# A two-layer attention kernel: the second scores of a layer-0 row placed behind the attention product of the row before

## The chip, the cores and the metric

The kernel runs on one core of one Trainium2 chip. Its engines are named as the profile names them: PE (TensorE, the matrix engine) with PEld (its weight loads), DVE (VectorE), ACT (ScalarE), POOL (GpSimd) and SP (SyncE, which issues most DMAs). The metric is the device time of one execution in microseconds (us). Beside plain timed runs there is one profiled execution, in which every instruction has a start and an end; its "span" is the time from the first to the last instruction.

## What is computed

The input x has 128 rows of 256 tokens with 256 channels, all float32. Two attention layers follow each other, each on a group-normalised copy of its input and with a residual. Layer 0, the one that is changed here, has 8 heads of 32 channels:

```python
bias = jnp.einsum('nijz,zh->nhij', pair_repr, bias_proj)[:, None]
gate = jax.nn.sigmoid(msa_repr @ gate_proj).reshape(bs, s, r, head, c)
q, k, v = jnp.split(msa_repr @ qkv_proj, 3, axis=-1)
...
sim = jnp.einsum('nsqhc,nskhc->nshqk', q, k) * scale
sim = jax.nn.softmax(sim, axis=-1)
sim = sim + bias
attend = jnp.einsum('nshqk,nskhc->nsqhc', sim, v) * gate
out = attend.reshape(bs, s, r, cm) @ out_proj
```

The bias is added after the softmax. So the attention output of a row is the sum of two products with v: the softmax weights with v, and the bias with v. Layer 1 has 4 heads of 64 channels and looks only at keys within 16 tokens of the query; the change doesn't touch it.

## The kernel before

The kernel has three stages: an early one (statistics of x, the bias table, weights turned into place), layer 0, and layer 1. Layer 0 goes row by row, `s` from 0 to 128 (lines 823 to 850), as a software pipeline: in step `s` the scores of row `s` are made, the attention of row `s - 1` is finished, and the projections of a later pair of rows are made.

Inside `tc.manual_schedule` (line 814) the order in which the source issues instructions is the order on PE, ACT and DVE; POOL and SP are not in its list. In a step PE gets, in order:

- `scores(s, 0)`: the scores of heads 0 to 3. Each product has 32 channels to sum over and 128 keys by 256 queries to write, a tile of 32x128 of PE's array ("32\*128" in the profile), and four heads stand side by side. Eight products, 16 matmul instructions (a float32 product is two passes), written `sim`, line 702. ACT then takes four exponentials (`ex`, line 713), each 128x512.
- `sum_heads(s - 1)`: the softmax sums of the row before (`zs`, line 743, 8 products) and the product of the bias with v (`bv`, line 729, 16 products). These sum over 128 keys and write 32 channels: tiles of 128x32 ("128\*32").
- `scores(s, 1)`: heads 4 to 7, as the first.
- `attend(s - 1)`: the product of the exponentials with v (`av`, line 729 too, 16 products), 128x32 tiles again. DVE then forms `at` (lines 774 to 777) from `bv`, `av`, the sums `z` and the reciprocal `d` that `divide` prepared.
- `stretch(...)`: the projections of a pair of rows with whole-array products ("128\*128"): q and k in even steps, v and the gate in odd ones. Each of the two (`f` and `g` in `sevens`, line 595) is made by seven products of half matrices instead of eight, accumulated in its own PSUM bank and copied out by ACT in between: product 1 and 5 and a copy "15" (line 580), product 2 of both into a shared bank (`twos`), then products 3, 6, 7, 4 with further copies. Product 3 accumulates onto what copy "15" has to have read. Between the last of these the output projection of row `s - 1` (`po`, line 634) is interleaved; it needs `at`.

PSUM has eight banks. Three are for `z`, `bv` and `av`; the other five are one ring (line 329, `psum(banks0, "0", 5, 0)`), from which the score tiles `sim`, the banks of the stretch and `po` are taken in turn: four sims, four sims, f's bank, g's bank, the shared bank, po. So each takes over the bank that was handed out five places earlier: f's bank was that of the last sim of `scores(s, 0)`, g's bank and the shared bank were those of the first and second sim of `scores(s, 1)`, and the first sim of `scores(s, 1)` takes that of the `po` of the step before, which DVE's sum into `o` (line 788) has to have read.

ACT's order in a step is: four exponentials of `scores(s, 0)`, the copy of `zs` into `z` (line 756), in even steps the exponential of the gate (line 831), four exponentials of `scores(s, 1)`, then the copies of the stretch. DVE's order is: one join of exponentials (line 719), `d` and its reciprocal (lines 758 and 759), the three operations of `at`, the other three joins, the minimum of z, the normalisation of a later row, and the output sum `o` with its statistics.

Of the kernel before, what the change touches and what calls it, by code (L numbers as in the profile page):

```python
# [39 lines left out]
def conv_preact_kernel(  # L40
# [608 lines left out]
    with ExitStack() as both:  # L649
# [6 lines left out]
        def load1(g):  # L656
            if g * XG < S and g not in ygs:
                yg = big1.tile([P, XG, 2, R], F32, tag="yg", name=f"yg{g}", bufs=5)
                nc.sync.dma_start(out=yg, in_=rows(x1, g * XG, XG))
                ygs[g] = yg  # L660

        with ExitStack() as lay0:
            row = lay0.enter_context(tc.tile_pool(name="row0", bufs=2))
            att = lay0.enter_context(tc.tile_pool(name="att0", bufs=2))
            st, hd, outs = {}, {}, {}
# [5 lines left out]
            def normal(s):  # L671
                if s >= S:
                    return
                g, k = ROWS[s]
                if k == 0:
                    load(g + 1)
                xt = row.tile([P, 2, R], F32, tag="xt", name=f"xt{s}", bufs=6)
                turned(xt, xgs[g], k)
                st[s] = {"xt": xt}
                i, r = divmod(s, 2)  # L680
                if r == 0:
                    xns[i] = row.tile([P, 4, R], F32, tag="xn", name=f"xn{i}")
                for half in range(2):
                    nc.vector.tensor_scalar(  # L684
                        xns[i][:, 2 * r + half, :], xt[:, half, :],
                        mean0[:, half : half + 1], rstd0[:, half : half + 1],
                        op0=ALU.subtract, op1=ALU.mult,
                    )

            def sum_rows(i):  # L690
                if 2 * i < S:
                    tss[i] = row.tile([P, 4, R], F32, tag="ts", name=f"ts{i}", bufs=1)
                    row_sums(tss[i], xns[i])

            def scores(s, half):
                i, r = divmod(s, 2)
                q, k = res["q", i], res["k", i]
                sims = [sim_bank(f"sim{s}_{half}_{j}") for j in range(4)]
                for kt in range(2):
                    for j in range(4):  # L700
                        p0 = D0 * j
                        nc.tensor.matmul(  # L702
                            sims[j][:, kt, :],
                            lhsT=k[p0 : p0 + D0, 2 * r + half, kt * P : (kt + 1) * P],
                            rhs=q[p0 : p0 + D0, 2 * r + half, :],
                            start=True, stop=True,
                        )
                ex = att.tile([P, 4, 2, R], F32, tag="ex", name=f"ex{s}_{half}", bufs=4)
                both = att.tile([P, 4, R], F32, tag="both", name=f"both{s}_{half}")
                hd[s, half] = (ex, both)  # L710

                for j in range(4):
                    nc.scalar.activation(ex[:, j], sims[j], AF.Exp, scale=1.0 / math.sqrt(D0))  # L713

            def join_tiles(s, half, j):

                if s < S:
                    ex, both = hd[s, half]
                    nc.vector.tensor_tensor(both[:, j : j + 2], ex[:, j : j + 2, 0, :], ex[:, j : j + 2, 1, :], ALU.add)  # L719

            def products(to, s, weights):

                i, r = divmod(s, 2)
                v = res["v", i]
                for half in range(2):
                    for kt in range(2):
                        for j in range(4):
                            c0 = kt * P + j * D0
                            nc.tensor.matmul(  # L729
                                to[D0 * j : D0 * (j + 1), half, :],  # L730
                                lhsT=v[:, 2 * r + half, c0 : c0 + D0], rhs=weights(4 * half + j, kt),
                                start=(kt == 0), stop=(kt == 1),
                            )

            def sum_heads(s):
                if s < 0:
                    return
                zs = ps_av.tile([P, 2, R], F32, tag="z", name=f"zs{s}")
                bv0 = ps_av.tile([P, 2, R], F32, tag="bv", name=f"bv{s}")
                for half in range(2):  # L740
                    both = hd[s, half][1]
                    for j in range(4):
                        nc.tensor.matmul(  # L743
                            zs[D0 * j : D0 * (j + 1), half, :], lhsT=ones[:, 0:D0], rhs=both[:, j, :],
                            start=True, stop=True,
                        )
                products(bv0, s, lambda h, kt: bias_sb[:, kt, h, :])
                hd[s] = bv0
                return zs
# [12 lines left out]
            def least(s, z):  # L762
                if s >= 0:
                    nc.vector.tensor_reduce(zmin[:, s : s + 1], z, axis=AX.XY, op=ALU.min)

            def attend(s):
                if s < 0:
                    return
                (ex0, _), (ex1, _), bv0 = hd.pop((s, 0)), hd.pop((s, 1)), hd.pop(s)
                av = ps_av.tile([P, 2, R], F32, tag="av", name=f"av{s}")  # L770
                products(av, s, lambda h, kt: (ex0, ex1)[h // 4][:, h % 4, kt, :])
                z, d = hd.pop((s, "z"))
                t = att.tile([P, 2, R], F32, tag="t", name=f"t{s}", bufs=1)
                nc.vector.tensor_tensor(t, bv0, z, ALU.mult)
                nc.vector.tensor_tensor(t, av, t, ALU.add)
                at = row.tile([P, 2, R], F32, tag="at", name=f"at{s}", bufs=1)
                nc.vector.tensor_tensor(at, t, d, ALU.mult)  # L777
                st[s]["at"] = at
# [18 lines left out]
            def stretch(names, i, s):  # L797

                po = iter(())
                if s >= 0:  # L800
                    po = one_by_one(out_sb, st[s]["at"], f"po{s}", lambda ps: st[s].update(po=ps))
                if 2 * i >= S:
                    for _ in po:
                        pass
                    return
                f, g = (
                    Seven(row, quarters[w], xns[i], tss[i], f"{w}{i}", w, by_token=(w == "v")) for w in names
                )
                for w, p in zip(names, (f, g)):
                    res[w, i] = p.to  # L810
                sevens(row, f, g, f"{names}{i}", po)


            with tc.manual_schedule(engines={mybir.EngineType.PE, mybir.EngineType.Activation, mybir.EngineType.DVE}):
                for s in range(2):
                    normal(s)
                sum_rows(0)
                stretch("qk", 0, -1)
                for s in range(2, 4):
                    normal(s)  # L820
                stretch("vg", 0, -1)
                sum_rows(1)
                for s in range(S + 1):
                    if s < S:
                        scores(s, 0)
                    zs = sum_heads(s - 1)
                    join_tiles(s, 0, 0)
                    divide(s - 1, zs)
                    if s % 2 == 0 and s < S:
                        e = res["g", s // 2]  # L830
                        nc.scalar.activation(e, e, AF.Exp, scale=-1.0)
                    if s < S:
                        scores(s, 1)
                    z = hd[s - 1, "z"][0] if s > 0 else None
                    attend(s - 1)
                    for half, j in ((0, 2), (1, 0), (1, 2)):
                        join_tiles(s, half, j)
                    least(s - 1, z)
                    if s == 4:
                        for weights in quarters1.values():  # L840
                            weights.sum()
                    if s == S - 1:
                        most1 = join_most(st1, stats1, 1)
                        load1(0)
                        load1(1)
                    stretch(("qk", "vg")[s % 2], s // 2 + 1, s - 1)
                    normal(s + 4)
                    if s % 2 == 1:
                        sum_rows((s + 3) // 2)
                    finish(s - 1)  # L850
# [6 lines left out]
        with ExitStack() as lay:  # L857
# [3 lines left out]
            st, hd, outs = {s: {} for s in range(S)}, {}, {}  # L861
# [403 lines left out]
```

## Time and profile before

| | us |
|---|---|
| median of 3 runs | 3258.2 |
| lowest and highest | 3253.23 and 3259.37 |
| profiled execution | 3257.72 |
| its span | 3256.0 |

The groups of the profile that belong to the lines concerned (the columns after the name: shapes, count, then busy us and mean ns of one instruction, then idle time of the engine before it and what ended it):

```profile
L713 ACT ACTIVATE ex<-sim 128x512 f32<-128x512 f32 x1024 | 527.4, 601 | 249.8 <-PE sim L702 249.8
...
L702 PE MATMUL sim<-q,k 32*128 32x256 f32 x4096 | 295.7, 401 | 1.1 <-ACT ex L713 1.1
...
L729 PE MATMUL av<-ex,v 128*32 128x256 f32 x4096 | 247.5, 382 | 0.0
...
L729 PE MATMUL bv<-bias_sb,v 128*32 128x256 f32 x4096 | 244.5, 379 | 0.0
```

A timeline of the profile merges like instructions that follow each other: its columns are the start, the time from the first start to the last end, the engine, the line, the operation, the tiles written and read, the form, the number of instructions, and in brackets the idle time before it and what ended that.

### The profile page before, as it was taken

Reading aid. Unit: us, or ns where it says so; the run is one execution under the profiler, and the core shown is the slowest. Engines: PE = TensorE matmul, PEld = TensorE weight load, DVE = VectorE, ACT = ScalarE, POOL = GpSimd, SP = SyncE. Lnnn points to the kernel's source line nnn. Section 1 sums busy time; section 2 is a strip of 40 time slices with the busy share of each in tenths; the row PEclk is TensorE's granted clock in tenths of the full one; section 3 lists DMA queues with packets and bytes.
Section 4 is the critical chain, followed back from the end, with each engine's and each line's share of the span. In section 5 each row is a group of like instructions: output and inputs, shape, how many; then the busy total and the mean of one; then the engine's idle time right before and its main releaser. Section 6 shows DMA issues by size and latency. Waiting matters only on the chain.

```text
span 3256.0 us, 86773 instructions
## 1 busy us (share of the span) xinstructions
PE 3151.5 (97%) x36937; PEld 2442.3 (75%) x36937; DVE 2678.8 (82%) x3547; ACT 2041.1 (63%) x4306; POOL 1683.4 (52%) x1657
## 2 busy tenths in 40 slices
PE   6799999999999999999999999799999999999997
PEld 4567777777777777777777777588888888888886
DVE  4759999999999999999999999857777777776667
ACT  4566666666666666666666666466666666665663
POOL 3034444444444444444444444287777777776774
PEclk9999999999999999999999999899999999999999
DMA  9931111111111111111111110012222222222221
GB/s 386 414 89 53 53 34 41 35 39 34 40 37 37 34 40 37 37 34 40 40 34 37 37 40 27 21 28 63 57 67 67 67 55 65 67 67 53 61 59 48
DMA packets 346330, 209.36 MB, mean 64 GB/s; under 512 B 273608, under 2 KB 339152, under 8 KB 339664
## 3 DMA queue, kind: packets, MB, share of 16 engines
q1 hardware_dynamic: 345040, 201.37, 21.2%
q8 instruction: 292, 4.78, 0.6%
q0 software_dynamic: 752, 2.36, 0.2%
q14 instruction: 102, 0.84, 0.1%
q10 hardware_dynamic: 144, 0.00, 0.0%
HBM read 136.59 MB, written 67.11 MB: 63 GB/s over the span
## 4 chain that ended last, share of the span: by engine, by line
PE 92%; DMA 3%; DVE 3%; issue 1%; ACT 0%; POOL 0%; SPq 0%; DVEq 0%; ACTq 0%
PE sim L702 8%; PE p1v L917 7%; PE av L729 7%; PE 1po L634 7%; PE po L634 7%; PE bv L729 7%; PE pv L569 6%; PE pq L565 6%; PE p1q L565 5%; PE pk L565 5%; PE p1k L565 5%; PE pg L565 5%; PE zs L743 4%; DMA xs<-in_x_dram 3%; PE 1sim L938 3%; PE 1avz L970 2%
## 5 line engine op out<-in xcount | busy, mean ns | idle before, releaser
L998 DVE RECIPROCAL 1rz<-1z 128x512 f32<-128x512 f32 x128 | 427.8, 3342 | 319.5 <-ACT 1z L992 319.5
L713 ACT ACTIVATE ex<-sim 128x512 f32<-128x512 f32 x1024 | 527.4, 601 | 249.8 <-PE sim L702 249.8
L719 DVE TENSOR_TENSOR both<-ex 128x512 f32<-128x512 f32 x512 | 484.1, 984 | 77.9 <-ACT ex L713 77.9
L759 DVE RECIPROCAL d<-d 128x512 f32<-128x512 f32 x128 | 429.2, 3353 | 4.4
L592 POOL TENSOR_TENSOR v<-v,twovg 128x256 f32<-128x256 f32 x64 | 72.8, 1137 | 551.3 <-ACT twovg L608 551.3
L634 PE MATMUL po<-at,out_sb 128*128 128x256 f32 x1024 | 288.3, 385 | 12.1 <-DVE at L777 12.1
L702 PE MATMUL sim<-q,k 32*128 32x256 f32 x4096 | 295.7, 401 | 1.1 <-ACT ex L713 1.1
L634 PE MATMUL 1po<-1at,w_out_t 128*128 128x256 f32 x1024 | 271.5, 389 | 5.0 <-DVE 1at L1004 3.1
L702 PEld LDWEIGHTS sim<-q,k 32*128 32x128 f32 x4096 | 186.6, 184 | 102.4 <-issue 69.4
L729 PE MATMUL av<-ex,v 128*32 128x256 f32 x4096 | 247.5, 382 | 0.0
L948 POOL TENSOR_TENSOR 1p<-1ex,seen 128x768 f32<-128x768 f32 x128 | 232.7, 1818 | 23.3 <-ACT 1ex L946 23.3
L729 PE MATMUL bv<-bias_sb,v 128*32 128x256 f32 x4096 | 244.5, 379 | 0.0
L917 PEld LDWEIGHTS p1v<-w_in_t,1xn 128*64 128x64 f32 x4096 | 223.6, 137 | 22.0 <-issue 22.0
L917 PE MATMUL p1v<-w_in_t,1xn 128*64 128x128 f32 x4096 | 239.1, 275 | 1.1 <-DVE 1xn L883 1.1
L634 PEld LDWEIGHTS 1po<-1at,w_out_t 128*128 128x128 f32 x1024 | 191.1, 192 | 54.6 <-ACT 1z L992 20.4
L634 PEld LDWEIGHTS po<-at,out_sb 128*128 128x128 f32 x1024 | 187.9, 194 | 34.4 <-issue 7.7
L592 POOL TENSOR_TENSOR q<-q,twoqk 128x256 f32<-128x256 f32 x64 | 47.2, 737 | 298.5 <-ACT twoqk L608 298.5
L729 PEld LDWEIGHTS av<-ex,v 128*32 128x32 f32 x4096 | 120.1, 109 | 108.2 <-issue 42.1
L729 PEld LDWEIGHTS bv<-bias_sb,v 128*32 128x32 f32 x4096 | 133.1, 110 | 87.9
L684 DVE TENSOR_SCALAR xn<-xt,mean,rstd 128x256 f32<-128x256 f32 x256 | 196.8, 808 | 0.0
L593 POOL TENSOR_TENSOR 1q<-1q,mid1q 128x512 f32<-128x512 f32 x64 | 81.6, 1274 | 191.2 <-ACT 1q L589 191.2
L955 POOL TENSOR_TENSOR 1zp<-1p 128x512 f32<-128x512 f32 x128 | 162.6, 1270 | 10.0
(259 smaller groups left out, 7638.3 us busy)
## 6 DMA issues: line engine op xcount, KB each, us to landing
pr<-in_L_conv_pair_repr_dram SPq DMA_DIRECT2D x32, 1024.0 KB, 22.9
x<-o SPq DMA_DIRECT2D x64, 512.0 KB, 2.8
yg<-x SPq DMA_DIRECT2D x64, 512.0 KB, 4.3
out_dram<-1o SPq DMA_DIRECT2D x256, 128.0 KB, 4.3
xg<-in_x_dram SPq DMA_DIRECT2D x252, 128.0 KB, 3.1
xs<-in_x_dram SPq DMA_DIRECT2D x15, 2048.0 KB, 21.8
xs<-in_x_dram SPq DMA_DIRECT2D x2, 1024.0 KB, 17.5
qkv_sb<-in_L_conv_qkv_proj_dram POOLq DMA_DIRECT2D x4, 192.0 KB, 12.2
```

The lines of the kernel that those rows point to most:

```text
L565: nc.tensor.matmul(out, lhsT=weights, rhs=moving, start=first, **flags)
L569: nc.tensor.matmul(out[:, cols], lhsT=moving[:, cols], rhs=weights, start=first and t2 == 0, **flags)
L634: nc.tensor.matmul(ps[:, m, :], lhsT=w[:, kt, m * P : (m + 1) * P], rhs=at[:, kt, :], start=(kt == 0), stop=(kt == 1),)
L684: nc.vector.tensor_scalar(xns[i][:, 2 * r + half, :], xt[:, half, :], mean0[:, half : half + 1], rstd0[:, half : half + 1], op0=ALU.subtra ...
L702: nc.tensor.matmul(sims[j][:, kt, :], lhsT=k[p0 : p0 + D0, 2 * r + half, kt * P : (kt + 1) * P], rhs=q[p0 : p0 + D0, 2 * r + half, :], sta ...
L713: nc.scalar.activation(ex[:, j], sims[j], AF.Exp, scale=1.0 / math.sqrt(D0))
L719: nc.vector.tensor_tensor(both[:, j : j + 2], ex[:, j : j + 2, 0, :], ex[:, j : j + 2, 1, :], ALU.add)
L729: nc.tensor.matmul(to[D0 * j : D0 * (j + 1), half, :], lhsT=v[:, 2 * r + half, c0 : c0 + D0], rhs=weights(4 * half + j, kt), start=(kt == ...
L759: nc.vector.reciprocal(d, d)
L917: nc.tensor.matmul(ps[KB * half : KB * (half + 1), b, :], lhsT=xns[i][:, 2 * r + kt, KB * b : KB * (b + 1)], rhs=w_in_t[:, kt, 2 * C + P * ...
L948: nc.gpsimd.tensor_tensor(p.rearrange("p j (r c) -> p (j r) c", c=WROW)[:, :, 0 : 2 * WSTEP] .rearrange("p r (t c) -> p r t c", c=WSTEP)[: ...
L998: nc.vector.reciprocal(st[s]["rz"], st[s]["z"])
```

## The change

Two calls in the step of layer 0 change places: `attend(s - 1)` is called ahead of `scores(s, 1)`. The line that looks up `z` moves along, since `attend` takes the entry out of its table. Nothing else is changed.

```diff
                     if s % 2 == 0 and s < S:
                         e = res["g", s // 2]
                         nc.scalar.activation(e, e, AF.Exp, scale=-1.0)
+                    z = hd[s - 1, "z"][0] if s > 0 else None
+                    attend(s - 1)
                     if s < S:
                         scores(s, 1)
-                    z = hd[s - 1, "z"][0] if s > 0 else None
-                    attend(s - 1)
                     for half, j in ((0, 2), (1, 0), (1, 2)):
                         join_tiles(s, half, j)
                     least(s - 1, z)
```

## The prediction

> **What bounds the kernel now.** First the page: the span, the engines, and the chain of work that ended last.
>
> ```profile
> span 3256.0 us, 86773 instructions
> PE 3151.5 (97%) x36937; PEld 2442.3 (75%) x36937; DVE 2678.8 (82%) x3547; ACT 2041.1 (63%) x4306; POOL 1683.4 (52%) x1657
> ...
> PE 92%; DMA 3%; DVE 3%; issue 1%; ACT 0%; POOL 0%; SPq 0%; DVEq 0%; ACTq 0%
> ```
>
> TensorE is the chain for 92% of the span. Two views then narrow it to the stage that is changed, layer 0 from its second row on (221 to 2080 us): the busy time of that stretch, and PE's waits in it.
>
> ```profile
> 221.00:2080.00 1859.00, 1855.62 (x19504) 1359.22 (x19503) 1732.01 (x2001) 1206.00 (x2451) 808.70 (x750) 1.00 0.14 37
> ```
>
> ```profile
> PE po L634 <- DVE at L777: 3.4, 1, 3.4
> ```
>
> The columns are PE, PEld (weight loads), DVE, ACT, POOL. PE is without a matmul for 3.4 us in 1859, and that is one wait at the stage's end. So time can come only from inside what counts as PE busy. The timeline of PE over one even row shows where (start, length, then the group; each 128x256 product is two passes):
>
> ```profile
> 1004.41 1.15 PE L702 MATMUL sim<-q,k 32*128 32x256 f32 x16
> 1005.48 1.07 PE L743 MATMUL zs<-both,ones 128*32 128x256 f32 x16
> 1006.37 1.91 PE L729 MATMUL bv<-bias_sb,v 128*32 128x256 f32 x32
> 1008.21 1.15 PE L702 MATMUL sim<-q,k 32*128 32x256 f32 x16
> 1009.28 1.93 PE L729 MATMUL av<-ex,v 128*32 128x256 f32 x32
> 1011.15 0.70 PE L565 MATMUL pq<-xn,qkv_sb 128*128 128x256 f32 x2
> 1011.68 0.59 PE L565 MATMUL pq<-ts,sums_q 128*128 128x256 f32 x2
> 1012.12 0.59 PE L565 MATMUL pk<-xn,qkv_sb 128*128 128x256 f32 x2
> ...
> 1013.84 0.59 PE L565 MATMUL pq<-xn,sums_q 128*128 128x256 f32 x2
> ```
>
> Read starts, not lengths, since lengths overlap. Undisturbed, two passes take 0.432 (1011.68 to 1012.12), so one takes 0.216, and four small tiles side by side take the time of one. That gives an ideal for each group, from its start to the next start. zs: 4 passes, 0.86, took 0.89. bv: 8 passes, 1.73, took 1.84. Each sim: 0.86, took 1.07 and 1.07. av: 1.73, took 1.87. The first pq: 0.43, took 0.53. The excess stands only where the tile form changes: about 0.11 on leaving a form, and on entering one 0.02 (128x32) or 0.10 (32x128 and 128x128). There are five changes in a row of 14.71 us (1004.41 to the next row's start at 1019.12).
>
> **What the Trainium skill says.** "TensorEngine Tiling (Array Packing)", section "Tiling Modes", says that a change of tiling mode, not of tile alone, drains TensorE. The trace agrees and gives the price: bv follows zs in the same mode without excess, every change costs about 0.13 to 0.21. "TensorE: Matmul & The Clock Gate", Part 2, says that a next weight load is pulled ahead of running matmuls; here the timeline of weight loads agrees inside a mode (pk's at 1011.90, its matmul at 1012.12), and at a change shows the loader idle 0.33 to 0.41 before it and the load uncovered. "Perfetto Trace Analysis", on the tensor engine's instructions, says that PE's end times are modelled; hence starts.
>
> **The change part by part.** The built programs show PE's order alone altered: sim(0), zs, bv, av, sim(1), stretch. DVE, ACT, POOL and SP issue the same instructions in the same order, so no instruction or DMA is added or passed over on any of them. It acts in rows 1 to 127 (row 0 has no av, row 128 no scores).
>
> 1. One mode change goes. Before, bv, sim(1), av take 1.84 + 1.07 + 1.87 = 4.78. After: bv 1.73, since av follows in its mode; av 1.73 + 0.11 for leaving to sim = 1.84; sim(1) 1.07, if leaving to the 128x128 products costs what leaving to av did; together 4.64. pq's own 0.10 on entering stays. Gain 0.14 a row. The steady trace has no change from sim to 128x128; row 0 has one, but at half clock (two passes take 0.85 there, 213.84 to 214.69): the first pq starts 0.07 before the last sim's modelled end (209.84 + 3.05 = 212.89 against 212.82), and the sim-to-zs change at full clock stands alike (1004.41 + 1.15 = 1005.56 against 1005.48). I take equal cost; leaving cost 0.10 to 0.14 wherever it is seen, so I allow 0.05 either way.
>
> 2. The cover between sim(1) and the products goes, and this is new. The stretch's banks come from the ring that sim uses. Its third product in f's bank accumulates onto what ACT's first copy ("15") must have read, and that copy is queued on ACT behind the four exponentials of sim(1). Before, av's 1.87 us stood between. These lines time the ACT side: an odd row's sim and exponentials; four exponentials and the next ACT operation; and a wait of PE on ACT from the start of the stage.
>
> ```profile
> 1022.92 1.15 PE L702 MATMUL sim<-q,k 32*128 32x256 f32 x16
> ...
> 1024.08 2.07 ACT L713 ACTIVATE ex<-sim 128x512 f32<-128x512 f32 x4 [1.17 <-PE sim L702]
> ```
>
> ```profile
> 1020.28 2.07 ACT L713 ACTIVATE ex<-sim 128x512 f32<-128x512 f32 x4 [1.33 <-PE sim L702]
> 1022.21 0.63 ACT L756 ACTIVATE z<-zs 128x512 f32<-128x512 f32 x1
> ```
>
> ```profile
> 219.62 0.37 ACT L574 COPY midk<-pk 128x256 f32<-128x256 f32 x1 [0.49 <-PE pk L565]
> ```
>
> ```profile
> 219.42 0.59 PE L565 MATMUL pq<-ts,sums_q 128*128 128x256 f32 x2
> 220.05 0.70 PE L565 MATMUL pk<-ts,sums_k 128*128 128x256 f32 x2
> 220.59 0.66 PE L565 MATMUL pq<-ts,sums_q 128*128 128x256 f32 x2
> ```
>
> The exponentials start 1.16 after sim(1); the next ACT operation starts 1.93 after their start, before the fourth has ended, so the copy starts at sim + 3.09. It takes 0.59 (all 128x512 copies of the stretch); ends at + 3.68. PE goes on about 0.05 after an ACT end (219.62 + 0.37 = 219.99, PE 220.05), and a load issued so late costs another 0.10 (220.05 to 220.59 is 0.54, not 0.43). So the third product works from sim + 3.83 or 3.84. PE is there at sim + 1.07 + 2.69 = 3.76 in an even row (1011.15 to 1013.84), and at 1.07 + 2.74 = 3.81 in an odd one, where the same places of the timeline are 1025.86 and 1028.60. Stall 0.07 and 0.02. The fourth exponential of a batch is 0.02 longer than the others; if the copy behind it is too, the stalls are 0.09 and 0.04. The middle is 0.08 and 0.03.
>
> 3. The other waits of the stretch on these exponentials: g's bank needs the first one (ends at sim + 1.76, plus 0.15; g starts at + 2.04), the shared bank the second (+ 2.25 plus 0.15; starts at + 2.91). Both are met. Behind the stalled product ACT catches up: its third copy ends near sim + 4.7, and the next copy can start only when PE's fourth f product ends, near + 4.9. So the stall is paid once a row.
>
> 4. What gets more room or stays. sim(1)'s bank from DVE's output sum of the row before is asked for 1.8 us later. DVE's at is set by the reciprocal (3.35 us), not by av: at is written by 1014.85, asked for at 1016.00 in the even row; 1029.42 against 1030.80 in the odd one. A row shortened by 0.1 leaves over 1.0 us. The sums for the next zs are done at 1017.72, asked for at 1020.19. All of these are hidden as before; if at's cushion were gone, each 0.1 us more on DVE would be 0.1 on PE.
>
> The sum for a pair of rows: 0.14 x 2 - 0.08 - 0.03 = 0.17 us; 63.5 pairs make 10.8 us. The profiled execution took 3257.72 us, of which 3256.0 are span; it stands 0.5 below the median of three, 3258.2. It would become 3246.9, and the median 3247.4; I say 3247. A measurement of this kernel cannot tell 0.2% (6.5 us) from no change.
>
> **The rivals.**
> - No stall. The release or the copy is 0.05 to 0.1 quicker than worked out, or the late load is covered. For it: at 220.59 the two passes lasted 0.66 instead of 0.59, so a load that comes only a little late costs only 0.07. Then 127 x 0.14 = 17.8 us: 3240.4.
> - The stall eats the gain. The copy comes 0.05 to 0.08 later, or leaving sim for 128x128 costs 0.05 more, and between 0.05 and 0.1 is lost per row: 3253 to 3258. Against it: every term is measured in this stage.
> - Slower: ACT doesn't overlap a copy with the fourth exponential. The trace shows an overlapped Identity behind them (1022.21), never a copy behind an exponential. The copy would then start at the fourth's end: sim + 1.16 + 2.07 = 3.23, end at 3.82, work from 3.97; stalls 0.21 and 0.16, against gains of 0.14. A pair loses 0.09, all of it 5.7 us; with 0.05 for the hand-over between the two, 12 us: about 3264 to 3270. It decides once the copy is over 0.1 us later than in part 2. Against it: four copies in a row in the first stage take 2.05 us for four of 0.59, so copies do overlap copies.
> - That the change does nothing on PE is excluded by the built order.
>
> **How the numbers follow.** My forecast (3244 to 3251) has 0.57, no stall 0.18, eaten 0.16, slower 0.09. The range reaches from just under the no-stall case, 3240, into the eaten case, 3254, and leaves out the slower case, half of the eaten one and a little below. Faster by over 0.2%: 0.57 + 0.18 = 0.75; within: 0.16; slower: 0.09.
>
> **What would show it.** In PE's timeline av starts 1.73 after bv, sim(1) is followed by the first stretch product at 1.07, and the row shrinks from 14.71 to about 14.65 (even) and from 14.81 (1019.12 to 1033.93) to about 14.70 (odd). In the stretch, the third product of f comes 2.77 after the first instead of 2.69 to 2.74, released by ACT's first copy, and that copy starts 3.09 after sim(1). I am wrong if that product waits over 0.14, if another product of the stretch waits, if sim to 128x128 costs over 0.1 more, or if po waits for at.

## The result and the profile after

The changed kernel takes 3249.93 us in the median of 12 runs (3247.23 to 3253.68); the kernel before, run beside it, 3257.81 us (12 runs, 3252.68 to 3263.71). The ratio is 0.9978, with a 95% interval of 0.9969 to 0.9987: 7.9 us faster, where 10.8 us was forecast. The profiled execution went from a span of 3256.0 to 3248.1 us.

From the page of the changed kernel: the span, the busy time of the engines, the chain of work that ended last, and the group of the exponentials (count, busy us, mean ns of one, idle time before it):

```profile
span 3248.1 us, 86776 instructions
...
PE 3145.8 (97%) x36937; PEld 2446.5 (75%) x36937; DVE 2670.0 (82%) x3547; ACT 2009.9 (62%) x4306; POOL 1685.0 (52%) x1657
...
PE 92%; DMA 4%; DVE 3%; issue 1%; ACT 0%; POOL 0%; SPq 0%; DVEq 0%; ACTq 0%
...
L713 ACT ACTIVATE ex<-sim 128x512 f32<-128x512 f32 x1024 | 528.7, 604 | 432.5 <-PE sim L702 432.5
```

The bound is the same: PE, 92% of the chain. The fourth line is the change at work on ACT: its idle time until `sim` rose from 249.8 to 432.5 us, since the second scores now come later in the row. Such a number is no cost by itself; whether it is depends on who waits for what ACT does next. The timeline of PE shows that, over one even row:

```profile
1001.15 1.15 PE L702 MATMUL sim<-q,k 32*128 32x256 f32 x16
1002.23 1.07 PE L743 MATMUL zs<-both,ones 128*32 128x256 f32 x16
1003.11 1.91 PE L729 MATMUL bv<-bias_sb,v 128*32 128x256 f32 x32
1004.84 1.91 PE L729 MATMUL av<-ex,v 128*32 128x256 f32 x32
1006.68 1.15 PE L702 MATMUL sim<-q,k 32*128 32x256 f32 x16
1007.76 0.70 PE L565 MATMUL pq<-xn,qkv_sb 128*128 128x256 f32 x2
...
1010.45 0.69 PE L565 MATMUL pq<-xn,sums_q 128*128 128x256 f32 x2
1010.98 0.59 PE L565 MATMUL pq<-ts,sums_q 128*128 128x256 f32 x2
```

Read the starts again: `bv` to `av` 1.73, `av` to `sim` 1.84, `sim` to the first product 1.08; together 4.65 in place of 4.78 (4.64 before the starts are rounded, so 0.14 less). That is the gain of one change of form. Then the price. The third product of q, at 1010.45, still starts 2.69 after the first, but the next one follows it after 0.53. In the kernel before that was 0.43:

```profile
1013.84 0.59 PE L565 MATMUL pq<-xn,sums_q 128*128 128x256 f32 x2
1014.27 0.59 PE L565 MATMUL pq<-ts,sums_q 128*128 128x256 f32 x2
```

In an odd row the same two starts lie 0.49 apart in the changed kernel (first two lines) and 0.44 in the one before:

```profile
1025.16 0.66 PE L569 MATMUL pv<-sums_v,xn 128*128 128x128 f32 x4
1025.65 0.61 PE L569 MATMUL pv<-sums_v,ts 128*128 128x128 f32 x4
...
1028.60 0.61 PE L569 MATMUL pv<-sums_v,xn 128*128 128x128 f32 x4
1029.04 0.61 PE L569 MATMUL pv<-sums_v,ts 128*128 128x128 f32 x4
```

So the lost time shows inside the third product, between its passes, and not in its start. ACT's timeline and the waits of the weight loads (who waits for whom, us in total, times, longest) name the cause:

```profile
1007.84 2.06 ACT L713 ACTIVATE ex<-sim 128x512 f32<-128x512 f32 x4 [1.16 <-PE sim L702]
1009.77 0.62 ACT L580 COPY q<-pq 128x512 f32<-128x512 f32 x1
```

```profile
PEld pq L565 <- ACT q L580: 14.1, 62, 0.2
PEld pv L569 <- ACT v L580: 11.5, 63, 0.2
```

The copy "15" (line 580) starts straight behind the fourth exponential, before that one has ended (1007.84 + 2.06 = 1009.90), ends at 1010.39, and the weights of the third product are loaded after that, at 1010.44. The wait view lists idle time of the loader, not loss. In the stretch a load starts 0.21 ahead of its product (1013.63 for 1013.84 in the kernel before); here the load is 0.20 later than that, and this lead hides about half of it. The loss is in the starts. Both waits are new; before, neither stood in the list.

A row, from one start of `zs` to the next in PE's timeline, is a precise ruler here, since all even rows of a kernel agree to 0.01 us, and all odd ones too, except for the first and last row, a single row in some kernels, and the odd rows of one kernel. The rows are those of the profiled execution. Each kernel's ratio is to runs of the kernel before beside it, whose medians were 3257.78 to 3258.63 us:

| kernel | even row | odd row | median us | ratio to before (95%) |
|---|---|---|---|---|
| before | 14.71 | 14.82 | 3257.81 | |
| changed | 14.67 | 14.73 | 3249.93 | 0.9978 (0.9969 to 0.9987) |
| late exponential | 14.57 | 14.68, half of them 14.92 | 3249.35 | 0.9973 (0.9964 to 0.9983) |
| the same, DVE's order kept | 14.57 | 14.68 | 3239.75 | 0.9950 (0.9937 to 0.9964) |
| av split | 14.71 | 14.82 | 3257.52 | 1.0000 (0.9992 to 1.0009) |
| fifth exponential, changed | 15.29 | 15.35 | 3328.8 | 1.0217 (1.0203 to 1.0231) |
| fifth exponential, before | 14.71 | 14.82 | 3254.97 | 0.9990 (0.9982 to 0.9999) |
| a join first | 14.91 | 14.73 | 3264.15 | 1.0022 (1.0013 to 1.0031) |

A pair of rows became 0.13 us shorter (29.53 to 29.40); 63.5 pairs make 8.3 us, against 7.9 us between the medians. So the rows account for the result.

### The profile page after: what moved, and what is told of

It is laid out like the page before. It is cut to its first block, busy times and chain, and to the rows that moved or that the text cites. A ratio compares the mean times of both kernels' runs of the same rounds, so it can differ in the third digit from the quotient of the medians.

```text
span 3248.1 us, 86776 instructions
## 1 busy us (share of the span) xinstructions
PE 3145.8 (97%) x36937; PEld 2446.5 (75%) x36937; DVE 2670.0 (82%) x3547; ACT 2009.9 (62%) x4306; POOL 1685.0 (52%) x1657
## 3 DMA queue, kind: packets, MB, share of 16 engines
q8 instruction: 292, 4.78, 0.6%
## 4 chain that ended last, share of the span: by engine, by line
PE 92%; DMA 4%; DVE 3%; issue 1%; ACT 0%; POOL 0%; SPq 0%; DVEq 0%; ACTq 0%
PE sim L702 8%; PE p1v L917 7%; PE po L634 7%; PE 1po L634 7%; PE bv L729 7%; PE av L729 7%; PE pq L565 6%; PE pv L569 6%; PE p1q L565 5%; PE pk L565 5%; PE p1k L565 5%; PE pg L565 5%; PE zs L743 4%; DMA xs<-in_x_dram 4%; PE 1sim L938 3%; PE 1avz L970 2%
## 5 line engine op out<-in xcount | busy, mean ns | idle before, releaser
L713 ACT ACTIVATE ex<-sim 128x512 f32<-128x512 f32 x1024 | 528.7, 604 | 432.5 <-PE sim L702 432.5
L729 PEld LDWEIGHTS av<-ex,v 128*32 128x32 f32 x4096 | 133.1, 110 | 88.0
L684 DVE TENSOR_SCALAR xn<-xt,mean,rstd 128x256 f32<-128x256 f32 x256 | 188.8, 777 | 0.0
```

The lines of the kernel that those rows point to most:

```text
L684: nc.vector.tensor_scalar(xns[i][:, 2 * r + half, :], xt[:, half, :], mean0[:, half : half + 1], rstd0[:, half : half + 1], op0=ALU.subtra ...
L729: nc.tensor.matmul(to[D0 * j : D0 * (j + 1), half, :], lhsT=v[:, 2 * r + half, c0 : c0 + D0], rhs=weights(4 * half + j, kt), start=(kt == ...
```

## The experiments

The theory: the change saves one change of tile form, 0.14 us a row, and gives part of it back because f's third product waits for ACT's copy, which now stands behind four exponentials with nothing in between on PE. There are two rivals: that the gain has to do with `av` itself (sooner, or straight behind `bv`), and that the loss is a property of the 128x128 products after 32x128 tiles, not of ACT.

**The gain: is it the number of changes of form?** The second scores are put into the middle of `av` (the call at their old place goes, except in row 0):

```diff
...
-                products(av, s, lambda h, kt: (ex0, ex1)[h // 4][:, h % 4, kt, :])
+                ex = lambda h, kt: (ex0, ex1)[h // 4][:, h % 4, kt, :]
+                products(av, s, ex, (0,))
+                if s + 1 < S:
+                    scores(s + 1, 1)
+                products(av, s, ex, (1,))
```

> The changed kernel, with the second scores placed in the middle of the attention product: its first half ahead of them, its second half behind them. Theory: a row has five changes of form again, and half of av (0.86 us) covers the copy, so no product waits: rows of 14.71 and 14.81 us and the time of the kernel before, ratio 1.000. Rival (the gain comes from av running sooner or straight behind bv, not from the number of changes of form): about half of the gain or more stays, 0.9975 or lower with the stall gone.

PE's timeline of this kernel, an even row:

```profile
1008.20 1.91 PE L729 MATMUL bv<-bias_sb,v 128*32 128x256 f32 x32
1009.92 1.05 PE L729 MATMUL av<-ex,v 128*32 128x256 f32 x16
1010.90 1.15 PE L702 MATMUL sim<-q,k 32*128 32x256 f32 x16
1011.97 1.07 PE L729 MATMUL av<-ex,v 128*32 128x256 f32 x16
1012.98 0.70 PE L565 MATMUL pq<-xn,qkv_sb 128*128 128x256 f32 x2
...
1015.67 0.59 PE L565 MATMUL pq<-xn,sums_q 128*128 128x256 f32 x2
1016.10 0.59 PE L565 MATMUL pq<-ts,sums_q 128*128 128x256 f32 x2
```

Half of `av` is still straight behind `bv` and starts 1.19 us sooner than before (1.72 after `bv` instead of 2.91), yet nothing of the gain is left: the ratio is 1.0000 and the rows are those of before to the hundredth. `bv` to the first product takes 4.78 again. The gain belongs to the number of changes of form. The third product is followed after 0.43, so it isn't held up: half of `av` is cover enough.

**The loss: is it ACT's copy?** One exponential of the second scores is done twice, to the same values, so that ACT has one more operation ahead of the copy; once in the changed kernel, once in the one before:

```diff
                 for j in range(4):
                     nc.scalar.activation(ex[:, j], sims[j], AF.Exp, scale=1.0 / math.sqrt(D0))
+                if half == 1:
+                    nc.scalar.activation(ex[:, 3], sims[3], AF.Exp, scale=1.0 / math.sqrt(D0))
```

> The changed kernel, with the fourth exponential of the second scores done twice, so that ACT has one more 128x512 operation ahead of f's copy 15. Theory: the copy comes one operation's pitch later, 0.48 us, and PE's third product with it, in every one of 127 rows: 61 us more than the changed kernel, ratio to the kernel before 1.016. Rival (ACT does not set that product's start): ratio 0.9978 as without it.

> The kernel before, with the same doubled exponential. Theory: av's 1.87 us stand between the second scores and the stretch, so the copy ends about sim + 4.2 (even rows somewhat later, behind the gate's exponential) while the third product comes at sim + 5.63: the doubled operation is hidden, ratio 1.000. Rival (ACT is close to a bound of its own in a row): slower by up to 61 us, 1.019.

In the changed kernel every row grew by 0.63 us and the program by 79 us against the changed kernel without it; in the kernel before, the same operation cost nothing: its rows are unchanged but for one. (Its ratio of 0.9990 is a little under 1, but layer 0, from the first `bv` to the last `av`, took 1875.3 us in its profiled execution and 1875.1 in that of the kernel before, so the difference lies outside of the rows.) So after the change ACT stands on PE's path, and `av` had been its cover. The size was misjudged, 0.63 a row for 0.48. ACT's timeline of the changed kernel with the fifth exponential shows why:

```profile
1012.15 2.06 ACT L713 ACTIVATE ex<-sim 128x512 f32<-128x512 f32 x4 [1.49 <-PE sim L702]
1014.25 0.60 ACT L715 ACTIVATE ex<-sim 128x512 f32<-128x512 f32 x1
1014.74 0.58 ACT L580 COPY q<-pq 128x512 f32<-128x512 f32 x1
```

Operations on different tiles start 0.48 apart, overlapping. The fifth writes the tile of the fourth, and it starts only after the fourth has ended (1012.15 + 2.06 = 1014.21). That is a wait of the program: in the trace the fifth waits for a semaphore that ACT's own operations raise, in all 128 rows, while the exponentials before it wait for PE. PE's line for the product now shows the wait openly, since it has become longer than what the loader's lead hides:

```profile
1015.37 0.70 PE L565 MATMUL pq<-xn,sums_q 128*128 128x256 f32 x2 [0.45 <-ACT q L580]
```

**Taking the loss away.** The copy needs only f's first two products, which are done long before the exponentials are. So the fourth exponential is issued behind it; the join on DVE that reads the exponential is issued behind that:

```diff
             p.take("15")
+            if last is not None:
+                last()
+                last = None
...
-                for j in range(4):
+                def exp(j):
                     nc.scalar.activation(ex[:, j], sims[j], AF.Exp, scale=1.0 / math.sqrt(D0))
+                for j in range(3 + (half == 0)):
+                    exp(j)
+                def last():
+                    exp(3)
+                    join_tiles(s, 1, 2)
+                return last
...
-                    if s < S:
-                        scores(s, 1)
-                    for half, j in ((0, 2), (1, 0), (1, 2)):
+                    last = scores(s, 1) if s < S else None
+                    for half, j in ((0, 2), (1, 0)):
```

> The changed kernel, with the fourth exponential of the second scores issued on ACT behind f's copy 15 instead of ahead of it (and DVE's join that reads it one place later). Theory (the change saves one change of tile form, 0.14 us a row, and gives most of it back because f's third product waits for that copy): the copy now starts at sim + 2.60 and ends near + 3.2, so the third product no longer waits; the interval from f's first to its third product is 2.69 (even rows) and 2.74 (odd rows), and the whole 127 x 0.14 = 17.8 us is kept: ratio to the kernel before 0.9945. Rival (the product is late for another reason, for instance the first weights after 32x128 tiles): no difference from the changed kernel, 0.9978.

The third product is no longer held up (the next one follows it after 0.43 in even and 0.44 in odd rows), even rows take 14.57, and many odd rows 14.68: 0.14 less than before in each. But the total is 0.9973 where 0.9945 was expected, little better than the changed kernel: nearly half of the odd rows (29 of 63 in the profiled execution) took 14.92. The timeline of such a row, where it loses time:

```profile
1022.98 0.72 POOL L592 TENSOR_TENSOR v<-v,twovg 128x256 f32<-128x256 f32 x1 [8.30 <-ACT twovg L611]
1023.03 1.22 DVE L789 TENSOR_TENSOR at<-t,d 128x512 f32<-128x512 f32 x1
...
1024.40 0.67 PE L637 MATMUL po<-at,out_sb 128*128 128x256 f32 x2
```

`po` (line 637 here) comes 0.61 after the product before it (1023.79) instead of 0.44. It waited for `at` (in all 29 rows it starts 0.15 after the end of `at`), and `at` took 1.22 us instead of 0.69: it started 0.05 after an addition on POOL and ended 0.55 after that one's end. In the Trainium skill, "SBUF — State Buffer", section "SBUF: two separate sides", says that DVE and POOL share a pair of ports under an exclusive lock: when a DVE operation with two SBUF inputs meets a POOL operation that reads SBUF, the later one is blocked for the earlier one's whole length. The trace agrees: 1.22 is the 0.67 for which POOL's operation still ran, plus 0.55. Where `at` starts first it is the other way round, as in an even row of the same kernel:

```profile
1008.36 0.69 DVE L789 TENSOR_TENSOR at<-t,d 128x512 f32<-128x512 f32 x1
1008.40 1.23 POOL L592 TENSOR_TENSOR q<-q,twoqk 128x256 f32<-128x256 f32 x1 [4.21 <-ACT twoqk L611]
```

Now `at` keeps its 0.69, and POOL's addition takes 1.23 instead of 0.72. So it is in all rows of this profile: `at` is long where POOL's addition has started first, and nowhere else. If the two merely slowed each other, both would be longer.

`at` had also come late. The edit had put the minimum of z ahead of the last join on DVE, and from there the operations of DVE and POOL met at other places. So the next run puts only the minimum of z back behind the join:

```diff
                 def last():
                     exp(3)
                     join_tiles(s, 1, 2)
+                    least(s - 1, hd[s, "least"])
...
-                    least(s - 1, z)
+                    if s < S:
+                        hd[s, "least"] = z
+                    else:
+                        least(s - 1, z)
```

> As the run with the late exponential, but the minimum of z follows the last join again, so DVE has the order of the changed kernel. In the run before it, half of the odd rows took 14.92 instead of 14.68 us: po waited for at, whose operation took 1.22 instead of 0.69 us beside POOL's first addition of the stretch, and DVE's d had been late and long (1.22 instead of 0.72) beside POOL too. Theory (the two orders of DVE set where the operations of DVE and POOL meet): at comes earlier again, no row waits, rows of 14.57 and 14.68, ratio to the kernel before 0.9945. Rival (with the shorter rows DVE meets POOL at that place whatever its order, or the cushion of at is used up): rows of 14.92 among the odd ones again, ratio 0.997.

All odd rows take 14.68, all even ones 14.57, and the kernel takes 3239.75 us, 0.9950 (0.9937 to 0.9964) of the kernel before. That is 18.0 us less than the 3257.78 beside it; the whole gain was worked out as 127 x 0.14 = 17.8. It beats both kernels, and the rows account for it: layer 0, again from the first `bv` to the last `av`, took 1859.8 us here and 1867.7 with the late exponential alone, 8.0 us less, where the medians differ by 9.6. (The profiled execution with the late exponential alone was the fastest of its ten, 3241.34 us, and took 5.4 us less outside of layer 0 than the profiled one here; the rows of the other nine aren't known.) Its PE and ACT timelines in the row whose changed-kernel lines are above:

```profile
1004.87 0.70 PE L565 MATMUL pq<-xn,qkv_sb 128*128 128x256 f32 x2
...
1007.57 0.59 PE L565 MATMUL pq<-xn,sums_q 128*128 128x256 f32 x2
1008.00 0.59 PE L565 MATMUL pq<-ts,sums_q 128*128 128x256 f32 x2
```

```profile
1004.96 1.57 ACT L716 ACTIVATE ex<-sim 128x512 f32<-128x512 f32 x3 [1.16 <-PE sim L705]
1006.41 0.61 ACT L580 COPY q<-pq 128x512 f32<-128x512 f32 x1
1006.87 0.64 ACT L716 ACTIVATE ex<-sim 128x512 f32<-128x512 f32 x1
```

The copy ends at 1007.02, half a microsecond before the third product, and the fourth exponential after it hurts nobody: its readers on DVE come after `at`.

**The cushion of at.** The prediction counted on more than 1.0 us between the end of `at` and the start of `po`. One join of DVE is moved ahead of the operations of `at`:

```diff
                 z, d = hd.pop((s, "z"))
+                join_tiles(s + 1, 0, 2)
...
-                    for half, j in ((0, 2), (1, 0), (1, 2)):
+                    for half, j in ((0, 2), (1, 0), (1, 2))[s > 0 :]:
```

> The changed kernel, with one of DVE's joins (0.98 us) put between the reciprocal and the three operations of at, so that at is ready 0.98 us later. Theory (at has a cushion of about 0.9 us in even and 1.2 us in odd rows of the changed kernel): po waits about 0.1 us in even rows and not in odd ones, 0 to 10 us over the layer, ratio 0.998 to 1.001. Rival (the cushion is smaller than read, or DVE carries the delay on from row to row): 0.5 us or more a row, ratio 1.01 or above.

Odd rows are unchanged, even rows are 0.24 longer; 1.0022 is outside both expectations, 0.0012 above the upper end of the theory's. The row's timeline shows the same meeting as before:

```profile
1018.68 0.73 POOL L592 TENSOR_TENSOR q<-q,twoqk 128x256 f32<-128x256 f32 x1 [4.70 <-ACT twoqk L608]
1018.74 1.22 DVE L778 TENSOR_TENSOR at<-t,d 128x512 f32<-128x512 f32 x1
...
1020.11 0.67 PE L634 MATMUL po<-at,out_sb 128*128 128x256 f32 x2
```

At its usual 0.69 us, `at` would have ended at 1019.43 and `po` been on time at 1019.94; it ended at 1019.96. The join took 0.63 here, not the 0.98 read from three of them together, and `at` started 0.60 later than in the changed kernel. DVE didn't carry the delay from row to row: all even rows are equally long, and the odd ones are as before. So the cushion was real, but shorter in effect than the distance in the timeline, because `at` lengthens by 0.53 when it starts behind POOL's addition. No run took POOL's addition away, so that ports are what the two contend for is the page's word; that the one which starts second is held up is what the traces show.

## Why the prediction was right, point by point

- **The bound.** Right. PE was the chain before and after, and the gain came out of the rows, in which the profile shows no idle time of PE in either kernel.
- **Step 1, one change of form goes, 0.14 a row.** Right, and shown: `bv` to `av` took 1.73, `sim` to the first product 1.08 (1.07 forecast, on the assumption of equal cost for a change that the trace before had only at half clock), and the split kernel took the gain back whole.
- **Step 2, the stall.** Right in cause, and in which product it hits. The copy started at sim + 3.09 as worked out. The sign named for it didn't come: the third product was to start 2.77 after the first, but it starts 2.69 and 2.74 after it as before, and the delay lies between its start and the next product's. Mis-sized is one term of the sum: the copy behind the exponentials took 0.62 us, against 0.59 to 0.61 taken. With it the stall is 0.10 in even and 0.05 in odd rows (intervals of 0.53 for 0.43 and 0.49 for 0.44) where 0.08 and 0.03 stood, and a pair of rows gains 0.13 instead of 0.17: over 63.5 pairs 2.5 us of the 2.9 us by which the gain fell short.
- **Step 3, no other wait of the stretch.** Right: in PE's timeline every other product of the stretch starts as long after the one before it as it did (0.43 or 0.44).
- **Step 4, at keeps its cushion.** Right for this kernel: `po` waited nowhere but at the stage's end, as before. But the stated "over 1.0 us" is not what a later `at` may use up, and that wasn't tested by the change: with `at` 0.60 later `po` already waited in even rows.
- **The rivals.** "No stall" at 3240.4 is what the last version reached by another edit, at 3239.75. "The stall eats the gain" asked for a copy 0.05 to 0.08 later than worked out; it ended 0.03 later (sim + 3.71). "ACT doesn't overlap a copy with the fourth exponential" is refuted: copy at 1009.77, fourth exponential until 1009.90.

## What to carry to other kernels

On a kernel that PE bounds, as here, count the changes of tile form in a loop body and read each one's price from the starts of the groups on both sides; moving groups of one form together won that price here, 0.14 us a row. Then ask what the moved group had been covering: the work that now follows directly may be gated by an engine that used to have that time. Where a copy is the gate, look in its engine's queue for an operation ahead of it that nobody needs soon, and keep the order of the other engines as it was.

## What the runs showed of the hardware

- Leaving one tile form for another cost the same for every change of form that a row has, at full clock (next group 0.30 to 0.31 us after the last matmul's start instead of 0.22), `sim` to 128x128 among them.
- ACT starts operations of 128x512 on different tiles 0.48 us apart, a copy behind an exponential too, but the copy is then a little longer: 0.62 instead of 0.59 us. An operation that writes the tile of its predecessor came 0.15 us later still, by a wait that stands in the program.
- `at`, an operation on DVE with two inputs in SBUF, took 1.22 us instead of 0.69 where it started just after an addition on POOL; where it started just before, the addition took 1.23 instead of 0.72. Such meetings moved when one instruction changed its place in DVE's order, and made 8.0 us of difference in layer 0 between two kernels with medians of 3249 and 3240 us.
